# Pairing an even and the next odd feature in one PSUM slot, with one VectorE product over both

## The chip, the cores and the metric

One core of a Trainium2 chip runs the whole program. The metric is device time in microseconds (us); most executions of one kernel agree within 0.3%. Runs were taken on several chips, each kernel beside runs of the kernel before on the same chip.

## The reference

A batch of 4096 rows holds 32 features of 64 numbers each. For every pair i < j of features, the row of i is multiplied by a 64 x 64 matrix of that pair, and the product is multiplied by the row of j, element by element. There are 496 pairs, so each row gives 496 x 64 = 31,744 numbers, and the output is 520 MB.

```python
vi = inputs[:, i_idx, :]                       # (4096, 496, 64)
vj = inputs[:, j_idx, :]
vdotw = jnp.einsum('bpd,pde->bpe', vi, W)
inter = vdotw * vj
return inter.reshape(B, -1)                    # (4096, 31744) float32
```

## The kernel before

The rows go in 32 tiles of 128. A tile's x is loaded, transposed on PE (through PSUM and a ScalarE copy) and then multiplied with all weights, which stay in SBUF. Feature i needs (31 - i) x 64 output columns. An even i sits in rows 0 to 63 of the PE array and the odd i after it in rows 64 to 127. A PSUM slot, one of four of two banks each, holds up to 1024 columns of one i:

```python
psum = ctx.enter_context(tc.tile_pool(name="ps", bufs=4, space=bass.MemoryType.PSUM))
opool = ctx.enter_context(tc.tile_pool(name="o", bufs=5))
...
for s, group in enumerate(STORES):             # 10 stores a tile
    ...
    osb = opool.tile([P, max(store_w)], F32, tag="o", name=f"o_{t}_{s}")
    for p in group:                            # p: the pair (2p, 2p + 1)
        for c0 in range(0, width[2 * p], NPS):              # NPS = 1024
            live = []
            for h in range(2):
                i = 2 * p + h
                n = min(NPS, width[i] - c0)
                if n > 0:
                    pm = psum.tile([P, NPS], F32, tag="ps", name=f"pm_{t}_{i}_{c0}")
                    live.append((h, i, n, pm))
            for b0 in range(0, NPS, BANK):                  # BANK = 512
                for h, i, n, pm in live:
                    ...
                    nc.tensor.matmul(pm[:, b0:b1], xT[h * D : (h + 1) * D, ts(p, P)],
                                     w_sb[p][h * D : (h + 1) * D, c0 + b0 : c0 + b1], ...)
            for h, i, n, pm in live:
                ...
                nc.vector.tensor_tensor(osb[:, o : o + n], pm[:, :n], xt[:, xj : xj + n], ALU.mult)
    nc.sync.dma_start(out=out[ts(t, P), o0 : o0 + store_w[s]], in_=osb[:, : store_w[s]])
```

Of the kernel before, what the change touches and what calls it, by code (L numbers as in the profile page):

```python
# [1 line left out]

# [6 lines left out]

F32 = mybir.dt.float32  # L10
ALU = mybir.AluOpType

P = 128
NPS = 1024
BANK = 512

STORES = [[0], [1], [2], [3], [4], [5], [6], [7], [8, 9], [10, 11, 12, 13, 14, 15]]
PREFETCH_AT = 5


@with_exitstack
def pair_bilinear_kernel(
    ctx: ExitStack,
    tc: tile.TileContext,
    x: bass.AP,
    w: bass.AP,
    out: bass.AP,
    F: int,
    D: int,
):  # L30












    nc = tc.nc
    B = x.shape[0]
    NT = B // P
    NPR = F // 2

    width = [(F - 1 - i) * D for i in range(F)]
    off = [sum(width[:i]) for i in range(F)]
    woff = [sum(width[0 : 2 * p : 2]) for p in range(NPR)]  # L50
    store_w = [sum(width[2 * p] + width[2 * p + 1] for p in g) for g in STORES]

    const = ctx.enter_context(tc.tile_pool(name="const", bufs=1))
    xpool = ctx.enter_context(tc.tile_pool(name="x", bufs=3))
    xtpool = ctx.enter_context(tc.tile_pool(name="xT", bufs=2))
    opool = ctx.enter_context(tc.tile_pool(name="o", bufs=5))
    psum = ctx.enter_context(tc.tile_pool(name="ps", bufs=4, space=bass.MemoryType.PSUM))

    ident = const.tile([P, P], F32, tag="ident", name="ident")
    make_identity(nc, ident)  # L60

    def load_x(t):
        xt = xpool.tile([P, F * D], F32, tag="x", name=f"x_{t}")
        nc.scalar.dma_start(out=xt, in_=x[ts(t, P), :])
        return xt

    def transpose_x(xT, t, xt, g):

        n = NPS // P
        pt = psum.tile([P, NPS], F32, tag="ps", name=f"pt_{t}_{g}")  # L70
        for c in range(n):
            nc.tensor.transpose(pt[:, ts(c, P)], xt[:, ts(n * g + c, P)], ident)  # L72
        nc.scalar.copy(xT[:, ts(g, NPS)], pt)  # L73

    def new_xT(t):
        return xtpool.tile([P, NPR * P], F32, tag="xT", name=f"xT_{t}")

    xs = {0: load_x(0)}

    w_sb = []  # L80
    for p in range(NPR):
        wp = const.tile([P, width[2 * p]], F32, tag=f"w{p}", name=f"w{p}")
        nc.sync.dma_start(out=wp, in_=w[:, woff[p] : woff[p] + width[2 * p]])
        w_sb.append(wp)

    xs[1] = load_x(1)
    xTs = {0: new_xT(0)}
    for g in range(2):
        transpose_x(xTs[0], 0, xs[0], g)

    for t in range(NT):
        xt, xT = xs.pop(t), xTs.pop(t)
        if t + 2 < NT:
            xs[t + 2] = load_x(t + 2)
        for s, group in enumerate(STORES):
            if t + 1 < NT and s in (PREFETCH_AT, PREFETCH_AT + 1):
                if s == PREFETCH_AT:
                    xTs[t + 1] = new_xT(t + 1)
                transpose_x(xTs[t + 1], t + 1, xs[t + 1], s - PREFETCH_AT)
            o0 = off[2 * group[0]]  # L100
            osb = opool.tile([P, max(store_w)], F32, tag="o", name=f"o_{t}_{s}")
            for p in group:
                for c0 in range(0, width[2 * p], NPS):
                    live = []
                    for h in range(2):
                        i = 2 * p + h
                        n = min(NPS, width[i] - c0)
                        if n > 0:
                            pm = psum.tile([P, NPS], F32, tag="ps", name=f"pm_{t}_{i}_{c0}")
                            live.append((h, i, n, pm))  # L110
                    for b0 in range(0, NPS, BANK):
                        for h, i, n, pm in live:
                            b1 = min(b0 + BANK, n)
                            if b1 > b0:
                                nc.tensor.matmul(  # L115
                                    pm[:, b0:b1],
                                    xT[h * D : (h + 1) * D, ts(p, P)],
                                    w_sb[p][h * D : (h + 1) * D, c0 + b0 : c0 + b1],
                                    start=True,
                                    stop=True,  # L120
                                )
                    for h, i, n, pm in live:
                        o = off[i] - o0 + c0
                        xj = (i + 1) * D + c0
                        nc.vector.tensor_tensor(  # L125
                            osb[:, o : o + n], pm[:, :n], xt[:, xj : xj + n], ALU.mult
                        )
            nc.sync.dma_start(
                out=out[ts(t, P), o0 : o0 + store_w[s]], in_=osb[:, : store_w[s]]
            )  # L130


# [33 lines left out]
```

## Time and profile before

| What | Value |
|---|---|
| time, median of 4 runs | 1349.26 us (1348.79 to 1350.20) |
| matmul busy (PE) | 1281.7 us, 95% |
| weight load busy (PEld) | 666.9 us, 49% |
| VectorE busy (DVE) | 1169.4 us, 87%, in 1472 instructions |
| data queues of the DMA | 99.3% of the time of 16 engines, 417 GB/s |

The lines behind this table stand in the prediction. Two more: the first is from the page's queue list (packets, MB, share of 16 engines). The second is from the view of the output tensor, whose last line gives the time from a store's issue to its landing.

```profile
q8 instruction: 42, 0.69, 0.2%
...
DMA to landing us min/median/max: 6.4/13.8/18.0
```

I read the q8 row as the fetch of PE's instructions: 5376 weight loads and 5376 matmuls are 10,752 instructions, and 42 packets of 16 KB are exactly 64 bytes for each. It looks negligible. The second row says that a store waits long in the queue: its own 1.6 MB on average need about 4 us at 417 GB/s.

### The profile page before, as it was taken

Reading aid. Unit: us, or ns where it says so; the run is one execution under the profiler, and the core shown is the slowest. Engines: PE = TensorE matmul, PEld = TensorE weight load, DVE = VectorE, ACT = ScalarE, POOL = GpSimd, SP = SyncE. Lnnn points to the kernel's source line nnn. Section 1 sums busy time; section 2 is a strip of 40 time slices with the busy share of each in tenths; the row PEclk is TensorE's granted clock in tenths of the full one; section 3 lists DMA queues with packets and bytes.
Section 4 is the critical chain, followed back from the end, with each engine's and each line's share of the span. In section 5 each row is a group of like instructions: output and inputs, shape, how many; then the busy total and the mean of one; then the engine's idle time right before and its main releaser. Section 6 shows DMA issues by size and latency. Waiting matters only on the chain.

```text
span 1348.6 us, 13450 instructions
## 1 busy us (share of the span) xinstructions
PE 1281.7 (95%) x5376; PEld 666.9 (49%) x5376; DVE 1169.4 (87%) x1472; ACT 66.1 (5%) x65; POOL 0.7 (0%) x6
## 2 busy tenths in 40 slices
PE   7899999999999999999999999999999999999996
PEld 3454555545545545555455554554554545545553
DVE  5789898898988888988889988898889888898996
ACT  1000000000000000000000000000000000000000
POOL 0000000000000000000000000000000000000000
PEclk9999999999999999999999999999999999999999
DMA  9999999999999999999999999999999999999999
GB/s 387 429 427 428 424 425 422 421 429 422 423 418 413 426 418 419 418 411 419 423 413 420 422 419 417 413 421 412 419 422 425 418 405 422 410 426 409 420 397 382
DMA packets 53054, 562.91 MB, mean 417 GB/s; under 512 B 6016, under 2 KB 6400, under 8 KB 7936
## 3 DMA queue, kind: packets, MB, share of 16 engines
q1 hardware_dynamic: 48384, 528.50, 93.3%
q10 hardware_dynamic: 4608, 33.56, 6.0%
q8 instruction: 42, 0.69, 0.2%
q14 instruction: 20, 0.16, 0.0%
HBM read 41.94 MB, written 520.09 MB: 417 GB/s over the span
## 4 chain that ended last, share of the span: by engine, by line
PE 70%; DVE 16%; DMA 10%; issue 3%; DVEq 0%
PE pm L115 66%; DVE o L125 16%; DMA out_dram<-o 10%; PE pt L72 4%; DMA x<-in_x_dram 1%; DVEq L125 0%; DVEq L162 0%
## 5 line engine op out<-in xcount | busy, mean ns | idle before, releaser
L125 DVE TENSOR_TENSOR o<-pm,x 128x1024 f32<-128x1024 f32 (+15 forms) x1472 | 1169.4, 866 | 170.0 <-PE pm L115 152.0
L115 PE MATMUL pm<-w,xT 64*128 64x512 f32 (+6 forms) x4864 | 1214.4, 539 | 37.2 <-DVE o L125 35.2
L115 PEld LDWEIGHTS pm<-w,xT 64*128 64x128 f32 x4864 | 610.5, 186 | 622.7 <-DVE o L125 404.3
L73 ACT COPY xT<-pt 128x1024 f32<-128x1024 f32 x64 | 64.8, 1012 | 1216.2 <-PE pt L72 1180.0
L72 PE MATMUL pt<-ident,x 128*128 128x128 f32 x512 | 71.4, 284 | 20.1 <-DVE o L125 11.6
L72 PEld LDWEIGHTS pt<-ident,x 128*128 128x128 f32 x512 | 56.4, 143 | 49.4 <-DVE o L125 40.9
L73 ACT ACT_TABLE_LOAD x1 | 1.3, 1283 | 2.1 <-issue 2.1
masks.py:199 POOL TENSOR_SCALAR_AFFINE_SELECT ident<-ident 128x128 f32<-128x128 f32 x1 | 0.3, 293 | 0.1
masks.py:197 POOL MEMSET ident<- 128x128 f32 x1 | 0.2, 205 | 0.3 <-POOLq L158 0.3
L158 POOL MEMSET const-bfloat16-1.0<- 128x1 bf16 x1 | 0.1, 102 | 0.0
L158 POOL MEMSET const-uint8-127<- 128x1 uint8 x1 | 0.1, 102 | 0.0
L158 POOL MEMSET const-float32-0.0<- 128x1 f32 x1 | 0.1, 99 | 0.2 <-issue 0.2
L158 POOL MEMSET const-float32-1.0<- 128x1 f32 x1 | 0.1, 99 | 0.0
## 6 DMA issues: line engine op xcount, KB each, us to landing
out_dram<-o SPq DMA_DIRECT2D x32, 2112.0 KB, 14.9
out_dram<-o SPq DMA_DIRECT2D x32, 1952.0 KB, 13.6
out_dram<-o SPq DMA_DIRECT2D x32, 1824.0 KB, 13.9
out_dram<-o SPq DMA_DIRECT2D x32, 1728.0 KB, 13.9
out_dram<-o SPq DMA_DIRECT2D x32, 1696.0 KB, 14.5
out_dram<-o SPq DMA_DIRECT2D x32, 1568.0 KB, 14.8
out_dram<-o SPq DMA_DIRECT2D x32, 1440.0 KB, 15.0
out_dram<-o SPq DMA_DIRECT2D x32, 1312.0 KB, 14.0
```

The costliest lines, as they stand in the source:

```text
L72: nc.tensor.transpose(pt[:, ts(c, P)], xt[:, ts(n * g + c, P)], ident)
L73: nc.scalar.copy(xT[:, ts(g, NPS)], pt)
L115: nc.tensor.matmul(pm[:, b0:b1], xT[h * D : (h + 1) * D, ts(p, P)], w_sb[p][h * D : (h + 1) * D, c0 + b0 : c0 + b1], start=True, stop=True,)
L125: nc.vector.tensor_tensor(osb[:, o : o + n], pm[:, :n], xt[:, xj : xj + n], ALU.mult)
L158: nc = bacc.Bacc("TRN2", target_bir_lowering=False, num_devices=1)
```

## The change

The intent is to let PE and VectorE work in finer steps. A slot keeps its two banks, but holds 512 columns of the even i in one and 512 of the odd i in the other. PE can fill both halves as soon as one slot is free. Where the halves are equally long, one VectorE instruction multiplies both, reading and writing two runs; where they are not, there are two.

```diff
-                for c0 in range(0, width[2 * p], NPS):
+                for c0 in range(0, width[2 * p], BANK):
+                    pm = psum.tile([P, 2, BANK], F32, tag="ps", name=f"pm_{t}_{p}_{c0}")
+                    n = [max(0, min(BANK, width[2 * p + h] - c0)) for h in range(2)]
...                  (one matmul per half h, into pm[:, h, : n[h]])
+                    if n[0] == n[1]:
+                        nc.vector.tensor_tensor(
+                            runs(osb, o[0], o[1], n[0]),
+                            pm[:, :, : n[0]],
+                            runs(xt, xj[0], xj[1], n[0]),
+                            ALU.mult,
+                        )
+                    else:
...                  (one tensor_tensor per half)
+    def runs(tl, a, b, n):
+        ap = tl[:, a : a + n]
+        return bass.AP(ap.tensor, ap.offset, [list(ap.ap[0]), [b - a, 2], list(ap.ap[1])])
```

More of the change, by code (lines that the diff above doesn't have):

```diff
@@ L13 @@
 P = 128
-NPS = 1024
 BANK = 512
@@ L67, in transpose_x @@
     def transpose_x(xT, t, xt, g):
-        n = NPS // P
-        pt = psum.tile([P, NPS], F32, tag="ps", name=f"pt_{t}_{g}")
+        n = 2 * BANK // P
+        pt = psum.tile([P, 2 * BANK], F32, tag="ps", name=f"pt_{t}_{g}")
         for c in range(n):
             nc.tensor.transpose(pt[:, ts(c, P)], xt[:, ts(n * g + c, P)], ident)
-        nc.scalar.copy(xT[:, ts(g, NPS)], pt)
+        nc.scalar.copy(xT[:, ts(g, 2 * BANK)], pt)
     def new_xT(t):
@@ L102, in pair_bilinear_kernel @@
             for p in group:
-                for c0 in range(0, width[2 * p], NPS):
-                    live = []
+                for c0 in range(0, width[2 * p], BANK):
+                    pm = psum.tile([P, 2, BANK], F32, tag="ps", name=f"pm_{t}_{p}_{c0}")
+                    n = [max(0, min(BANK, width[2 * p + h] - c0)) for h in range(2)]
                     for h in range(2):
-                        i = 2 * p + h
-                        n = min(NPS, width[i] - c0)
-                        if n > 0:
-                            pm = psum.tile([P, NPS], F32, tag="ps", name=f"pm_{t}_{i}_{c0}")
-                            live.append((h, i, n, pm))
-                    for b0 in range(0, NPS, BANK):
-                        for h, i, n, pm in live:
-                            b1 = min(b0 + BANK, n)
-                            if b1 > b0:
-                                nc.tensor.matmul(
-                                    pm[:, b0:b1],
-                                    xT[h * D : (h + 1) * D, ts(p, P)],
-                                    w_sb[p][h * D : (h + 1) * D, c0 + b0 : c0 + b1],
-                                    start=True,
-                                    stop=True,
-                                )
-                    for h, i, n, pm in live:
-                        o = off[i] - o0 + c0
-                        xj = (i + 1) * D + c0
-                        nc.vector.tensor_tensor(
-                            osb[:, o : o + n], pm[:, :n], xt[:, xj : xj + n], ALU.mult
-                        )
@@ new lines, in pair_bilinear_kernel @@
+                        if n[h]:
+                            nc.tensor.matmul(
+                                pm[:, h, : n[h]],
+                                xT[h * D : (h + 1) * D, ts(p, P)],
+                                w_sb[p][h * D : (h + 1) * D, c0 : c0 + n[h]],
+                                start=True,
+                                stop=True,
+                            )
+                    o = [off[2 * p + h] - o0 + c0 for h in range(2)]
+                    xj = [(2 * p + h + 1) * D + c0 for h in range(2)]
@@ new lines, in pair_bilinear_kernel @@
+                    if n[0] == n[1]:
[4 more added lines that the diff above has]
+                            ALU.mult,
+                        )
+                    else:
+                        for h in range(2):
+                            if n[h]:
+                                nc.vector.tensor_tensor(
+                                    osb[:, o[h] : o[h] + n[h]],
+                                    pm[:, h, : n[h]],
+                                    xt[:, xj[h] : xj[h] + n[h]],
+                                    ALU.mult,
+                                )
```

## The prediction

> **What bounds the kernel now.** I read the page first for shares, then the DMA queues, then the waits of one tile of 128 rows, then the landings of the stores. The page of the kernel before says:
>
> ```profile
> PE 1281.7 (95%) x5376; PEld 666.9 (49%) x5376; DVE 1169.4 (87%) x1472; ACT 66.1 (5%) x65; POOL 0.7 (0%) x6
> ...
> GB/s 387 429 427 428 424 425 422 421 429 422 423 418 413 426 418 419 418 411 419 423 413 420 422 419 417 413 421 412 419 422 425 418 405 422 410 426 409 420 397 382
> DMA packets 53054, 562.91 MB, mean 417 GB/s; under 512 B 6016, under 2 KB 6400, under 8 KB 7936
> ## 3 DMA queue, kind: packets, MB, share of 16 engines
> q1 hardware_dynamic: 48384, 528.50, 93.3%
> q10 hardware_dynamic: 4608, 33.56, 6.0%
> ...
> PE pm L115 66%; DVE o L125 16%; DMA out_dram<-o 10%; PE pt L72 4%; DMA x<-in_x_dram 1%; DVEq L125 0%; DVEq L162 0%
> ```
>
> Three things look full at once: PE at 95%, VectorE (DVE) at 87%, and the two data queues of the DMA at 93.3 + 6.0 = 99.3% of the span. The chain of waits (last line) names PE, which tempts one to call this a PSUM ping-pong. The GB/s row is what makes me doubt it: no slice passes 429, and the mean is 417.
>
> The waits inside one tile that met no DMA wait (window 715.08 to 755.99 us, 40.91 us long), and the waits of VectorE over the whole run:
>
> ```profile
> DVE o L125 <- PE pm L115: 4.4, 4, 1.5
> ...
> DVE o L125 <- PE pm L115: 152.0, 125, 15.2
> DVE o L125 <- DMA out_dram<-o: 18.0, 22, 2.3
> ```
>
> In that tile VectorE idles four times, 4.4 us in all. Busy time of VectorE in the same window is 36.53 us, and 36.5 + 4.4 = 40.9. So the compute side alone can do a tile in **40.91 us**. The timeline shows two of those four stalls and an unbroken VectorE stretch:
>
> ```profile
> 721.08 19.11 DVE L125 TENSOR_TENSOR o<-pm,x 128x1024 f32<-128x1024 f32 x20 [1.48 <-PE pm L115]
> 741.27 1.22 DVE L125 TENSOR_TENSOR o<-pm,x 128x1024 f32<-128x1024 f32 x1 [1.08 <-PE pm L115]
> ```
>
> Against that stands the DMA. I took the issue and the landing of each of the 320 stores from the trace. A tile's last store lands 41.24 to 41.29 us after the previous tile's in tiles 3 to 8, and 41.40 to 41.63 us in tiles 13 to 27; over tiles 1 to 28 the mean is (1232.1 - 72.5) / 28 = 41.41 us. A tile moves 128 x 31744 x 4 B = 16.25 MB out and 1.05 MB in, so 17.30 MB in 41.24 us is 419 GB/s. Two to four stores are already in flight at each issue in those tiles, and a store takes 13.8 us (median) to land where its own bytes need about 4. The queue is never empty. So the DMA (41.4 us a tile) is already slower than the compute side (40.91), by only 1%, and VectorE pays the difference in its 22 waits for a free output buffer. The 16 increments of a store's semaphore also drift apart: first and last are 0.5 us apart at the start and 5 to 7 us in the middle. Some engines run ahead and now and then dry, and the slowest paces the kernel.
>
> Only in the last three tiles, when no x load is left, does compute bind: stores land 37.80, 38.06 and 39.89 us apart while issues are 40.90, 40.91 and 39.22 apart, and the backlog melts from 14 us to 8.
>
> **What the Trainium skill says.** "Perfetto Trace Analysis", section "Identifying the Most-Contended Engine": matmul busy time is no measure of distance to the roofline; look at weight-load busy time. The trace agrees: PE 95%, PEld 49%, and in the window above PEld waits 12.1 us for VectorE. The same page, section "What 'DMA-bound' means", lists specific DMA engines as one kind of bound; the landing skew fits that. "DMA: Bandwidth & Descriptors", section "Specifications", gives a fabric ceiling of 435 GB/s and an HBM limit of about 358 per core. The mean 417 and the best slice 429 agree with the first and lie above the second; the measurement decides. "Vector Engine (DVE) Microarchitecture Reference", section 5.2, gives 1.0417 ns per column and about 75 ns per instruction in a queue. The trace agrees: the stretch above holds 20 instructions and 16,960 columns; 16,960 x 1.0417 = 17.67 us, and (19.11 - 17.67) / 20 = 0.07 us each.
>
> **The change part by part.**
>
> 1. Instruction counts, from the built order. VectorE goes from 46 to 52 instructions a tile (1472 to 1664); equal chunks stay 1024 columns wide (2 x 512), but the uneven remainders are now cut at 512, which adds six. Cost: 6 x 0.07 = +0.4 us a tile, +13 us over 32 tiles if it all lay on the path. Columns, matmuls (76 a tile), transposes, copies, stores and loads stay the same. I expect the two runs of 512 to stream like one of 1024, since each run is long and unit-step; no run here shows it yet.
>
> 2. PSUM slots. Before, a slot held 1024 columns of one i, and the order even, odd, even, odd had to fill two slots before either multiply could go. In the trace the first big group starts at 719.07 us and its first multiply at 721.08: 2.0 us. One freed slot also served one half of the array only; the odd half's weight load then blocked the queue. After, one slot holds an even/odd pair. A pair of two 512-column matmuls is four PE instructions, which the trace runs at 0.165 and 0.264 us alternately, 0.86 us a pair; the multiply behind it takes 1.13 us from start to start (1024 x 1.0417 + 0.07). PE is faster than VectorE per slot and three slots deep ahead of it.
>
> 3. So the four stalls (4.4 us) should mostly go. By hand: at the tile's start, the last small slots give VectorE about 1.3 us of work while PE needs about 1.1 for the first pair; around a transpose group (1.09 us on PE, 1.01 on ScalarE) three slots hold about 3.3 us of work. I leave 0.7 us. The compute side becomes 31744 x 1.0417 = 33.1, plus 52 x 0.07 = 3.6, plus 0.7 = **37.4 us** a tile, 3.5 less than before.
>
> 4. What that is worth: the path is set by the DMA, whose bytes and stores are unchanged, so in tiles 1 to 28 nothing. The 3.5 us turn into waits for output buffers. In tiles 29 to 31 the stores can keep the DMA's own pace of about 37.9 us: 3 x 37.9 = 113.7 against 115.7 before, a gain of 2 us.
>
> Sum: tile 0 lands at 72.5 as before; 28 x 41.4 = 1159.2; 113.7; and 1.4 between the last landing (1347.8) and the median time (1349.2). Total 1346.8, which I round to **1346** because fuller queues should lose a little less to dry engines.
>
> **The rivals.**
>
> *Ping-pong is the bound.* If the chain of waits is right, every tile loses 3.5 us: 1349 - 32 x 3.5 = 1237. For it: the chain's 66% on PE and the 404 us in which PEld waits for VectorE. Against: 17.30 MB in 37.4 us is 463 GB/s, above every slice of the row. I give it 1%.
>
> *VectorE becomes the bound.* The six extra instructions, or two-run operands that stream slower, lengthen it: 1349 + 13 = 1362 for the first. Against: VectorE's work of 36.7 us leaves 4.7 us of room under 41.4. The two-run instructions hold 24,576 of the 31,744 columns (25.6 us), so they would have to be some 18% slower before it showed. 2% that the total grows by more than 2%.
>
> *Depth changes the DMA's pace.* With four stores always in flight, tiles could keep the 41.24 of tiles 3 to 8 (1342) or drift to the 41.57 of tiles 13 to 27 or a bit more (1352). This I cannot decide, and it makes the range.
>
> **Range and chances.** The two paces give 1342 to 1352; below I add 4 us for fewer dry engines (the DMA loses some 11 us to dips between its first and last microseconds). So 1338 to 1352. A change of 2% needs the DMA's rate itself to move: faster 0.01, same 0.97, slower 0.02.
>
> **What would show it.** Right: VectorE's wait for the output buffers rises from 18 us to some 90 to 150; its wait for PE falls from 152 to 20 to 60 (15 are the first load); VectorE x1664, busy 1175 to 1200 us; the chain of waits moves from PE to the stores (over 40%); median landing time rises from 13.8 to about 17 us, since five buffers at 41.4 / 10 us each less one being written (3.7) give 5 x 4.14 - 3.7; tile periods stay at 41.2 to 41.6, and the mean stays 415 to 421 GB/s. Wrong: a mean above 430 GB/s (then PSUM did bind), two-run multiplies clearly over 1.22 us, or VectorE still waiting for PE by over 100 us.

## The result, and the profile after

The changed kernel takes **1349.11 us** (median of 4 runs, 1347.65 to 1349.98) against 1349.26. The ratio is 0.9997, with a 95% interval of 0.998 to 1.0014: the same. (A ratio here is the mean time of one kernel's fast runs over that of the other's fast runs of the same rounds, so not quite the ratio of the medians.)

The page of the changed kernel, in the parts that answer to those shown of before:

```profile
PE 1150.9 (85%) x5376; PEld 513.4 (38%) x5376; DVE 1176.8 (87%) x1664; ACT 66.1 (5%) x65; POOL 0.7 (0%) x6
...
GB/s 386 428 430 425 424 425 423 423 426 422 422 420 413 429 419 417 420 418 419 426 412 418 403 423 425 422 417 405 424 415 413 423 422 419 405 425 422 412 425 364
DMA packets 53056, 562.93 MB, mean 418 GB/s; under 512 B 6016, under 2 KB 6400, under 8 KB 7936
## 3 DMA queue, kind: packets, MB, share of 16 engines
q1 hardware_dynamic: 48384, 528.50, 93.4%
...
DMA out_dram<-o 38%; DVE o L122 37%; DVE o L131 16%; DMA x<-in_x_dram 1%; PE pm L112 0%; PE pt L76 0%; DVEq L122 0%; DVEq L171 0%
```

Much moved and the time did not. PE fell from 95% to 85% busy. The chain that ended last ran 66% over PE's matmuls before; now PE has almost no share in it, VectorE has 53% (37 + 16) and the stores have 38%. Two rows stayed: VectorE's busy share, 87%, and the data rate, 417 GB/s before and 418 after.

The waits of VectorE (who waited for whom: us in total, times, longest), then its timeline around the middle of one tile, and the landing time of the stores:

```profile
DVE o L122 <- DMA out_dram<-o: 107.5, 89, 3.6
...
DVE o L122 <- PE pm L112: 50.4, 31, 14.4
...
730.78 3.47 DVE L122 TENSOR_TENSOR o<-pm,x 128x1024 f32<-128x1024 f32 x3
734.17 0.21 DVE L131 TENSOR_TENSOR o<-pm,x 128x64 f32<-128x64 f32 x1
735.62 2.35 DVE L122 TENSOR_TENSOR o<-pm,x 128x1024 f32<-128x1024 f32 x2 [1.24 <-DMA out_dram<-o]
737.89 1.08 DVE L131 TENSOR_TENSOR o<-pm,x 128x448 f32<-128x448 f32 x2
740.23 2.36 DVE L122 TENSOR_TENSOR o<-pm,x 128x1024 f32<-128x1024 f32 x2 [1.26 <-DMA out_dram<-o]
...
748.57 2.35 DVE L122 TENSOR_TENSOR o<-pm,x 128x1024 f32<-128x1024 f32 x2 [1.20 <-PE pm L112]
...
DMA to landing us min/median/max: 9.7/15.1/18.9
```

VectorE's idle time changed little in sum, 170 us before and 158 after. But by the view's labels 152 us of it were waits for PE, and 50 are now; 18 us were waits for an output buffer, and 107 are now. At the start of a store (735.62, 740.23) VectorE stands still until an older store has landed.

The labels even understate this. A wait for several things is put down to the one that the profile saw last. In the changed kernel, 28 of the waits put down to PE (34 us; the one at 748.57 is among them) end within 0.2 us of the landing of the store that held the buffer, just as the waits put down to stores do (0.12 us, median). Counted by landings, VectorE waits 142 us for buffers and 16 for PE, and 14 of these 16 are the wait for the first matmuls of the run. (In the kernel before, the same count moves only 4 us.) So most of the wait was not removed but moved from PE to the stores. Stores also queue longer, 15.1 us instead of 13.8.

### The profile page after: what moved, and what is told of

It reads as the page before. It is cut to its first block, busy times and chain, and to the rows that moved or that the text cites. A ratio compares the mean times of both kernels' runs of the same rounds, so it can differ in the third digit from the quotient of the medians.

```text
span 1347.7 us, 13642 instructions
## 1 busy us (share of the span) xinstructions
PE 1150.9 (85%) x5376; PEld 513.4 (38%) x5376; DVE 1176.8 (87%) x1664; ACT 66.1 (5%) x65; POOL 0.7 (0%) x6
## 4 chain that ended last, share of the span: by engine, by line
DVE 53%; DMA 38%; issue 7%; PE 1%; DVEq 0%
DMA out_dram<-o 38%; DVE o L122 37%; DVE o L131 16%; DMA x<-in_x_dram 1%; PE pm L112 0%; PE pt L76 0%; DVEq L122 0%; DVEq L171 0%
## 5 line engine op out<-in xcount | busy, mean ns | idle before, releaser
L112 PE MATMUL pm<-w,xT 64*128 64x512 f32 (+7 forms) x4864 | 1087.2, 550 | 173.8 <-DVE o L122 152.1
L122 DVE TENSOR_TENSOR o<-pm,x 128x1024 f32<-128x1024 f32 x768 | 900.9, 1213 | 158.1 <-DMA out_dram<-o 107.5
L112 PEld LDWEIGHTS pm<-w,xT 64*128 64x128 f32 x4864 | 457.1, 188 | 777.8 <-DVE o L122 532.6
L131 DVE TENSOR_TENSOR o<-pm,x 128x448 f32<-128x448 f32 (+6 forms) x896 | 327.6, 411 | 0.3 <-PE pm L112 0.3
## 6 DMA issues: line engine op xcount, KB each, us to landing
out_dram<-o SPq DMA_DIRECT2D x32, 1952.0 KB, 15.1
```

What stands on the lines that cost most here:

```text
L112: nc.tensor.matmul(pm[:, h, : n[h]], xT[h * D : (h + 1) * D, ts(p, P)], w_sb[p][h * D : (h + 1) * D, c0 : c0 + n[h]], start=True, stop=True,)
L122: nc.vector.tensor_tensor(runs(osb, o[0], o[1], n[0]), pm[:, :, : n[0]], runs(xt, xj[0], xj[1], n[0]), ALU.mult,)
L131: nc.vector.tensor_tensor(osb[:, o[h] : o[h] + n[h]], pm[:, h, : n[h]], xt[:, xj[h] : xj[h] + n[h]], ALU.mult,)
```

## The experiments

The theory is that the DMA sets the time of both kernels, and that the change made the compute side faster behind it. The first rival is that the change gains nothing on the compute side. A second question came up with the first runs: what makes the DMA slow down to 41.4 us a tile, when the best stretches are faster?

All "us a tile" below are counted from the landing of one tile's last store to that of a later tile, and averaged over tiles 1 to 28 unless said otherwise.

### Half of each store: the compute side laid bare

The same edit in both kernels halves the DMA's work and leaves PE and VectorE as they are. Half of the output is not written, so the result is wrong.

```diff
-                out=out[ts(t, P), o0 : o0 + store_w[s]], in_=osb[:, : store_w[s]]
+                out=out[ts(t, P), o0 : o0 + store_w[s] // 2], in_=osb[:, : store_w[s] // 2]
```

The kernel before:

> The kernel before, with only the first half of each store's columns written out (a wrong result on purpose; matmuls and multiplies complete). Bytes per tile fall from 17.3 to 9.2 MB, about 22 us of DMA. Theory (the DMA set the time, and the old PSUM slots cost about 4.4 us a tile behind it): the compute side shows itself, 15 us to the first multiply + 32 x 40.9 - 1.7 in the last tile + about 5 of tail = 1327 us; no VectorE wait for stores; VectorE still waits about 4.4 us a tile for PE. Rival (PSUM ping-pong was the bound of the full kernel all along): also about 1327, so this run alone does not decide; its pair does.

Measured: 1324.82 us, ratio to the full kernel 0.9814 (0.9799 to 0.9829).

The changed kernel:

> The changed kernel with half of each store (wrong on purpose). Theory (the change does speed the compute side, and the full DMA hid it): VectorE's 36.8 us of work and about 1.1 us of waits for PE give 37.9 us a tile, 15 + 32 x 37.9 + 5 = 1233 us, 7% below its pair. Rival (the change gives the compute side nothing, the gain in one place is paid for in another): within 1% of its pair, about 1327.

Measured: 1196.15 us, ratio to the full kernel before 0.8862 (0.8847 to 0.8876). Against its pair that is 1196.15 / 1324.82 = 0.903. It is 37 us below the expected 1233, which had counted 37.9 us a tile; a tile took 36.81.

The waits and one stretch of VectorE's timeline, first of the old slots, then of the new:

```profile
DVE o L125 <- PE pm L115: 151.0, 128, 14.0
...
545.81 19.11 DVE L125 TENSOR_TENSOR o<-pm,x 128x1024 f32<-128x1024 f32 x20 [1.48 <-PE pm L115]
566.00 3.09 DVE L125 TENSOR_TENSOR o<-pm,x 128x1024 f32<-128x1024 f32 x4 [1.08 <-PE pm L115]
570.43 2.82 DVE L125 TENSOR_TENSOR o<-pm,x 128x1024 f32<-128x1024 f32 x4 [1.34 <-PE pm L115]
```

```profile
DVE o L122 <- PE pm L112: 23.2, 31, 14.4
DVE o L122 <- DMA out_dram<-o: 0.2, 1, 0.2
...
552.19 2.36 DVE L122 TENSOR_TENSOR o<-pm,x 128x1024 f32<-128x1024 f32 x2 [0.29 <-PE pm L112]
```

The old slots stall VectorE at exactly the places and by the amounts (1.48, 1.08, 1.34 us) that the full kernel showed; the new ones by 0.29 us a tile. The tiles are issued 40.91 us apart in the one and 36.81 in the other. The theory holds and the first rival falls: the change is worth **4.1 us a tile, 10% of the compute side**. In the full kernel almost none of it shows. Halving the stores of the kernel before gained only 1.9%, since its compute side was close behind the DMA.

### The slots without the merged instruction

```diff
-                    if n[0] == n[1]:
+                    if False:
```

(in the changed kernel with half stores)

> As the last run, but each pair is multiplied out by two VectorE instructions: the slot layout without the merged instruction. 24 more instructions a tile at 0.07 us are 1.7 us. If the slot layout brings the gain: 15 + 32 x 39.6 + 5 = 1287 us. If the merged instruction is what brings it: about 1327, as with the old slots.

Measured: 1237.30 us, ratio to the full kernel before 0.9166 (0.9152 to 0.9179), 50 us below the 1287 expected for the layout; tiles are issued 38.10 us apart. All of VectorE's wait for PE is this one, before the first product of the run:

```profile
DVE o L131 <- PE pm L112: 13.5, 1, 13.5
```

Of the 4.1 us a tile, the slot layout brings 40.91 - 38.10 = 2.8 and the merged instruction 38.10 - 36.81 = 1.3. The 1.3 is not yet the price of 24 instructions: the merged kernel stalls 0.29 us a tile for PE, and this one does not. Without that stall it is 38.10 - (36.81 - 0.29) = 1.58 us, or 0.066 us each, close to the 0.07 that I had expected. The traces agree: back-to-back products start 1131 ns apart at 1024 columns and 598 ns apart at 512 (medians), and 2 x 598 - 1131 = 65 ns. The layout does not need the merged instruction.

### Loads and stores alone

PE, PSUM and the transposes are taken out. One VectorE instruction per store fills its buffer from a constant and the tile's x, so that stores and loads keep their order and dependences (a wrong result).

```diff
-            for p in group:
-                ...                      (matmuls and products)
+            n = store_w[s]
+            nc.vector.tensor_scalar(osb[:, :n], src[:, :n], xt[:, s : s + 1], None, ALU.mult)
```

> All loads and all stores as in both kernels, no PE, PSUM or ScalarE work; one VectorE scalar multiply per store fills its buffer (wrong on purpose), about 1,000 instructions in all. Theory (the DMA alone sets the time): 1320 to 1348 us, close to both kernels. Rival (the compute side sets a good part of it): well below 1310. A side theory on the spread of the landings: the 16 KB packets that fetch instructions (42 in the kernel before, one every 31 us, 0.94 us each) land on a few DMA engines and make these the slow ones; then here, almost without them, first and last landing of a store stay within 2 us and a tile takes about 40.6 us (1322 in all); if it is not the fetches, the spread grows to 5 to 7 us as before and the time is about 1345.

Measured: 1328.32 us, ratio 0.9842 (0.9828 to 0.9857), 40.73 us a tile. From its page and waits:

```profile
GB/s 387 431 426 431 424 425 423 424 430 425 425 424 422 428 424 423 425 424 423 429 427 422 424 423 430 425 424 424 426 419 430 422 425 425 422 429 425 430 428 398
...
q14 instruction: 11, 0.08, 0.0%
...
DVE o L83 <- DMA out_dram<-o: 702.7, 315, 17.8
```

With hardly any compute the kernel saves 1.6%. So a rearrangement of PE and VectorE work could hardly have gained more, as long as these bytes go this way. Here VectorE waits for a buffer before 315 of 320 stores; that is what a kernel wholly in the DMA's hands looks like.

There is a second finding. First and last of the 16 landings of a store stay 0.9 us apart here (median of tiles 9 to 28), where both full kernels show 6.0 us. And the q8 row is gone. That fits the side theory of the instruction fetches, which the next runs test.

### PE instructions that do no work

To the kernel above, 84 tiny matmuls a tile are added. PE then runs as many instructions as in the full kernels.

```diff
+            pm = psum.tile([P, 16], F32, tag="ps", name=f"pm_{t}_{s}")
+            for _ in range(9 if s < 4 else 8):
+                nc.tensor.matmul(pm, src[:, :P], osb[:, :16], start=True, stop=True)
```

> The loads-and-stores kernel (1328 us; a tile every 40.8 us; landings within 1.3 us of each other) plus a stream of 84 tiny matmuls a tile (16 columns each, wrong result as before), so that PE runs as many instructions as in both kernels and fetches as many (42 packets of 16 KB), while PE, PSUM and VectorE hardly touch memory. Theory (the fetch of PE's instructions makes a few DMA engines the slow ones): landings spread to 5 to 7 us, a tile takes 41.3 to 41.5 us, 1343 to 1349 us in all. Rival (it is the traffic of PE, VectorE and ScalarE on the on-chip memory that slows the DMA): no change from 1328 us.

Measured: 1343.29 us, ratio 0.9958 (0.9943 to 0.9973), 41.16 us a tile, landings 8.7 us apart. It is slower than loads and stores alone, as the theory wanted, but a tile is under its 41.3 to 41.5 us and the spread over its 5 to 7.

Then the dose, half as many again and smaller ones (`pm[:32], src[:32, :32], osb[:32, :16]`, 13 or 12 a store):

> The dose: 126 tiny matmuls a tile in place of 84 (each now 32 x 32 x 16), so about 63 fetches of 16 KB in place of 43. The 43 cost 41.16 - 40.73 = 0.43 us a tile; in proportion 63 cost 0.63, a tile takes 41.36 us and the whole 1349 us. If what slowed the last one was PE's own memory traffic and not the fetches: these matmuls read a quarter or less of it, so below 1343.

Measured: 1354.57 us, ratio 1.0038 (1.0023 to 1.0052), 41.53 us a tile, landings 9.2 us apart. The fetch rows of the two pages, in this order:

```profile
q8 instruction: 43, 0.70, 0.2%
```

```profile
q8 instruction: 64, 1.05, 0.3%
```

Instructions that compute nothing useful make the DMA slower: 0.43 us a tile with 43 fetches, 0.80 with 64 (more than the 0.63 expected in proportion). The matmuls of the second run read less memory but are more in number, and they cost more. So the loss goes with the number of PE instructions here and not with PE's traffic.

That the fetches are what does it is not shown. A fetch is one packet of 16 KB and takes about 0.94 us. A store has 16 landings and is complete with the last of them, so 0.2% of all packet time could cost 1% of the run if the packets held up the part that lands last. Then the step from one store's last landing to the next one's should be longer when a fetch falls into it. I compared steps of stores of the same size, with and without a fetch (205 steps of each trace, stores 80 to 284; +- is one standard error). In the kernel before, a fetch adds 0.35 +- 0.06 us. In the two runs above, which were to test the theory, it adds nothing: 0.04 +- 0.04 us with 43 fetches and 0.01 +- 0.02 us with 64. There every early step of a tile is longer by much the same share. The first two steps take 4.64 and 4.34 us in loads and stores alone, 4.73 and 4.42 with 43 fetches, 4.77 and 4.48 with 64 (medians of tiles 3 to 28). In the full kernels they are 4.66 and 4.35 before and 4.64 and 4.34 after, so these lose their time in other stores. Something that comes evenly with PE's instructions would fit the two runs better than 64 separate packets. The recording of each instruction for the profile is one untested candidate.

The landings do not settle it either. In the kernel before, about the middle of the run, some thirteen of a store's landings lie close together and two or three lag by 4 to 6 us; with the 43 fetches, late in the run, eight lag by 4 to 8.5 us. The trace doesn't tell which engine took a packet.

### On-chip traffic from few instructions

> The loads-and-stores kernel (1328 us, a tile every 40.7 us) plus on-chip traffic from few instructions: per store three ScalarE copies and one VectorE product of 1024 columns each, about 1,600 instructions more over the whole run, no PE. If such traffic slows the DMA: a tile takes 41 us or more, 1337 us or more. If only the fetches do: within 2 us of 1328, landings within 2 us of each other.

Measured: 1464.90 us, ratio 1.0855 (1.0837 to 1.0873). This run is no evidence. The added copies and products read a constant, so nothing kept them in step; they were ordered ahead of the stores, and the DMA ran short of stores, at 319 to 400 GB/s in many slices of the first part of the page. The second attempt ties them to each store's buffer:

```diff
+            for r in range(2):
+                nc.scalar.copy(scr, osb[:, 1024 * r : 1024 * (r + 1)])
+            nc.vector.tensor_tensor(scr2, osb[:, :1024], osb[:, 1024:2048], ALU.mult)
```

> The first attempt at this was spoilt: its extra work was not tied to the stores, was ordered ahead of them in bulk, and left the DMA without stores to move. Here each store's extra work (two ScalarE copies and one VectorE product of 1024 columns) reads that store's own buffer, so it stays in step. Some 21 us of ScalarE and 31 us of VectorE a tile, few instructions, no PE. If on-chip traffic slows the DMA: a tile over 41 us, above 1336 us. If only the fetches do: within 3 us of 1328 and landings within 2 us of each other.

Measured: 1330.58 us, ratio 0.9858 (0.9841 to 0.9874), 40.80 us a tile, landings 1.1 us apart. ScalarE is busy for 670 us and VectorE for 987, and the DMA does not mind: 0.07 us a tile. So, for traffic of this kind, memory contention is out as the cause.

### Fewer PE instructions in the changed kernel

Each of the 76 float32 matmuls of a tile is issued as two (76 x 32 x 2 = 4864 on the page). Here the matmuls read only the upper 16 bits of each number, as bf16, in one pass:

```diff
+    def top(ap):
+        b = ap.bitcast(mybir.dt.bfloat16)
+        return b.rearrange("p (n two) -> p n two", two=2)[:, :, 1]
...
-                                xT[h * D : (h + 1) * D, ts(p, P)],
-                                w_sb[p][h * D : (h + 1) * D, c0 : c0 + n[h]],
+                                top(xT[h * D : (h + 1) * D, ts(p, P)]),
+                                top(w_sb[p][h * D : (h + 1) * D, c0 : c0 + n[h]]),
```

> The changed kernel with its matmuls reading only the top 16 bits of each number (bf16 by truncation, a coarser result): one pass in place of two, so PE runs 5,888 instructions in place of 10,752, and fetches 23 packets of 16 KB. Stores, loads and VectorE's work are unchanged. Theory of the fetches: about 45% of the 0.65 us a tile comes back, 1338 to 1342 us. If PE's speed mattered to the full kernel: [...]far more than 1% would come. If neither matters: 1349.

Measured: 1340.50 us, ratio 0.9938 (0.9923 to 0.9953), 41.08 us a tile. It passes the comparison with the reference, with coarser products. From its page and waits:

```profile
PE 723.5 (54%) x2944; PEld 249.2 (19%) x2944; DVE 1176.9 (88%) x1664; ACT 66.1 (5%) x65; POOL 0.7 (0%) x6
...
q8 instruction: 23, 0.38, 0.1%
...
DVE o L128 <- PE pm L118: 51.0, 28, 12.7
```

PE's busy time falls from 1151 to 724 us; the granted TensorE clock was 0.51 in these runs, against 0.98 in the changed kernel. VectorE's waits put down to PE stay at 51 us, but 23 of these 28 end within 0.6 us of the landing of the store that held the buffer. So PE's speed had little part in the time. What came back is 41.47 - 41.08 = 0.39 us a tile with 19 fetches and 4864 PE instructions fewer (weight loads and matmuls), in the range that the theory of the fetches gave. A cause that goes with the number of instructions would give the same, and PE also reads only half of each number here; this run cannot separate them. The landings are still 5.5 us apart (6.0 in the changed kernel), so their spread does not follow the number of fetches.

This is the fastest version with all outputs written that passed. It is 0.6% below the kernel before, which by the rule of 2% counts as the same, at a price in precision that the change itself does not have; so I count it as evidence more than as a recommendation.

### Three output buffers instead of five

If the change makes the compute side quicker, it might pay where there is less slack between VectorE and the DMA.

```diff
-    opool = ctx.enter_context(tc.tile_pool(name="o", bufs=5))
+    opool = ctx.enter_context(tc.tile_pool(name="o", bufs=3))
```

The kernel before:

> The kernel before with 3 output buffers in place of 5, the full result. Filling a store's buffer takes 40.9 / 10 = 4.1 us on average, the DMA 4.14, and only two stores can be in flight; with hardly any slack between the two, every unevenness of store sizes[...] is paid for. Theory: 1400 us or more. Rival (buffers are not where the slack lies): 1349 to 1360.

Measured: 1424.58 us, ratio 1.056 (1.0534 to 1.0587).

The changed kernel:

> The changed kernel with 3 output buffers, the full result. Filling a buffer takes 36.8 / 10 = 3.7 us against 4.14 of the DMA, so some slack is left. Theory: 2 to 5% below its pair with the old slots, 1355 to 1385 us; here the change should show in the time. Rival: the same as its pair within 1%.

Measured: 1418.14 us, ratio 1.051 (1.0493 to 1.0528).

The chains that ended last, in shares by engine and line, first of the old slots and then of the new:

```profile
PE pm L115 49%; DVE o L125 23%; DMA out_dram<-o 20%; PE pt L72 4%; DMA w<-in_w_dram 2%; DVEq L125 0%; SPq L83 0%; DVEq L162 0%; SPq L128 0%
```

```profile
DMA out_dram<-o 57%; DVE o L122 24%; DVE o L131 14%; DMA w<-in_w_dram 2%; PE pm L112 1%; DVEq L122 0%; SPq L87 0%; DVEq L171 0%; SPq L137 0%
```

Both lose some 5%, and the gain of the change is 0.5%, not the 2 to 5% that I expected. My theory of this pair missed. The stretch of the changed kernel's windows (engine busy times; the last two columns are DMA share and GB/s) that ends one tile and begins the next suggests why:

```profile
615.00:620.00 5.00, 4.02 (x18) 1.20 (x14) 4.41 (x6) 0.00 (x0) 0.00 (x0) 1.00 1.01 428
620.00:625.00 5.00, 4.02 (x20) 1.59 (x20) 4.37 (x8) 0.00 (x0) 0.00 (x0) 1.00 0.90 380
625.00:630.00 5.00, 4.02 (x24) 2.18 (x22) 5.00 (x11) 0.00 (x0) 0.00 (x0) 1.00 0.85 359
630.00:635.00 5.00, 5.00 (x26) 2.74 (x26) 5.00 (x9) 0.00 (x0) 0.00 (x0) 1.00 0.81 293
```

The third busy column is VectorE: from 625 to 635 us it is fully busy, first with the last store of the tile (4224 columns) and then with the first of the next (3904), the two largest, and the DMA falls to 81%. There VectorE's own work is the limit, which the change does not shorten, and with two stores in flight the queue cannot bridge it. This is read from one stretch of one trace; no run tested it. Where the new slots save time, VectorE waits for a buffer instead: 183 us of waits for stores against 62 with the old slots. With five buffers the queue bridges it in both.

## Why the prediction was right

The measured 1349.1 us lie in the range of 1338 to 1352, and "the same" was given 97%. The parts of the sum hold one by one: tile 0 lands at 72.5 us as foreseen, a tile takes 41.47 us where 41.4 was put, and the last three take 113.2 where 113.7 was put. No two errors had to cancel.

1. *The DMA bounds the kernel, by 1%.* Shown. Loads and stores alone take 1328 us, 98.4% of the whole. Halving the stores uncovers a compute side of 40.91 us a tile, the very number read from one tile's waits before. For the changed kernel these two runs leave no doubt: compute alone takes 1196 us, the DMA alone 1328. For the kernel before they are a tie, 1325 and 1328. That the DMA set its pace rests on the queue: a store was in flight at every issue but the first, and tiles landed 41.41 us apart. The 1% comes only with PE at work, since the DMA alone needs 40.73 us a tile. The prediction took the 41.4 from the trace and had no cause for it.

2. *Cost of six more VectorE instructions.* Right: busy time went from 1169.4 to 1176.8 us (1175 to 1200 foreseen). The two-run instructions take 1213 ns on average, the old ones of 1024 columns 1216 ns, so two runs cost nothing. The price of an instruction is 0.065 us (half stores, with and without the merged instruction), where 0.07 was put.

3. *The four stalls go.* Right, and by more than I allowed: 0.3 us are left where I had left 0.7. The compute side is 36.81 us a tile, not 37.4.

4. *In tiles 1 to 28 nothing, in the last three tiles 2 us.* Right in both parts: 41.47 us a tile against 41.41, and 113.2 us for the last three against 115.7 (113.7 foreseen). Of these 2.5 us, 1.6 went again as 0.06 us a tile in the 28 before. All of this is of the size of the run-to-run spread.

5. *Fuller queues lose a little less to dry engines.* This did not come. (The 3 us between 1346 and the result are hardly more than the run-to-run spread.) The likely reason: at every issue after the first, in both kernels, an earlier store was still in flight, so the slowest engines had work all along, and only they set the pace. Keeping the fast ones fed gains nothing. My third rival, that queue depth changes the pace, is not what the runs point to first: with four stores always in flight the DMA made 40.73 us a tile alone and 41.16 with PE's instructions added.

Of the signs I named, the data rate (418 GB/s) and, by their labels, the waits (107 us for stores, 50 for PE) came within their ranges. Counted by landings the waits are 142 and 16 us, and the second is then below its 20 to 60. Three signs missed. The stores' share in the chain is 38%, not over 40%. Single tiles land 40.1 to 43.4 us apart, 11 of 28 outside 41.2 to 41.6 (3 of 28 in the kernel before); only their mean is inside. Landings take 15.1 us, not 17: that number supposed a wait before every store, as in the run of loads and stores alone (315 waits, median landing 18.1 us), but VectorE had to wait before 117 of 320 stores only (89 by the labels).

**What stays open.** With its 42 fetches the changed kernel takes 41.47 us a tile, and the stream of idle PE instructions with 43 fetches takes 41.16. These 0.3 us a tile, some 9 us in all, are not accounted for. By which way PE's instructions slow the DMA is open too, as told above. VectorE and ScalarE traffic made 0.07 of difference; PE's real operand traffic, the less steady arrival of the stores and the other instruction queue were not tested one by one.

## What to carry to other kernels

When several engines look full, compare rates before chains: bytes per tile over the time that a faster compute side would need must stay under the best rate that any of the page's 40 slices shows (here 463 GB/s wanted, 429 seen in 34 us), or the gain only renames the wait. Slices much shorter than a tile won't do: over 2.9 us this run shows up to 466. To see what a hidden change is worth, thin out the resource that hides it in both kernels: half stores showed 10% where the full kernels showed nothing. And in a kernel that is bound by DMA, count the PE instructions: here 10,752 of them that did no useful work cost 15 us of 1328, and 16,128 cost 26, by a way that is not known yet.

## What the Trainium skill lacked or had wrong

- "DMA: Bandwidth & Descriptors", section "Latency and other measured facts", says that some DMA engines are usually slower in traces and takes its best guess to be specific to the software descriptor path. These kernels issue all data transfers from the SP and ACT queues, and the 16 landings of a store still fell 6.0 us apart (median of tiles 9 to 28) with PE at work, and 0.9 us without.
- No page says that PE instructions which do no work slow the data transfers: 10,752 of them, with 43 fetches of 16 KB, raised the time from 1328.3 to 1343.3 us, and 16,128 with 64 fetches to 1354.6. It would belong to "Runtime: NRT & Kernel Launch", section "Instruction fetch mechanics", which says nothing of data transfers beside the fetches. That the fetches are the cause is not shown here.
- "DMA: Bandwidth & Descriptors", section "Specifications", lists an HBM limit of about 358 GB/s per core without the condition that its section "Bandwidth" adds further down (the other core of the pair streaming too). One core alone moved 417 GB/s here, and 424 with loads and stores only.
- "Vector Engine (DVE) Microarchitecture Reference", section 5.2, gives about 75 ns per queued instruction. Here it is 64 to 65 ns over 1.0417 ns a column: back-to-back products that read PSUM start 1131 ns apart at 1024 columns and 598 ns apart at 512.
